# Normalization factors by way of DRAM, and channel-major groups kept in place, in the projection stage of a compacted pair-mixing layer

## The chip, the core and the metric

One core of a Trainium2 chip runs the whole program. Its engines work side by side, each through its own list of instructions in order: PE (matmuls and transposes, into PSUM), DVE and ACT (elementwise work and reductions), POOL (elementwise work, and DMAs that it issues in software), SP (here only a DMA queue). They wait for each other by semaphores. The metric is the time of one execution on the device in microseconds, as the median of the runs shown.

## What is computed

The reference has two layers on an image x of 512 x 512 places with 64 channels. The change lies in the first:

```python
xn = _ln(gn(x), norm_w, norm_b)          # over the 64 channels of each place
left  = (xn @ left_w  + left_b)  * mask
right = (xn @ right_w + right_b) * mask
left  = left  * sigmoid(xn @ lgate_w + lgate_b)
right = right * sigmoid(xn @ rgate_w + rgate_b)
out_gate = sigmoid(xn @ ogate_w + ogate_b)
out = einsum('bkjd,bkid->bijd', left, right)
x = x + (_ln(out, onorm_w, onorm_b) @ out_w + out_b) * out_gate
```

`gn` is a group norm over the whole image, in effect one scale and one shift per channel. `mask[i, j]` is `m[i] * m[j]`, with m a vector of zeros and ones, so left and right are nonzero only where both row and column are kept. The second layer adds a filter in a few Fourier modes of the result.

## The kernel before

When at most K = 256 of the 512 indices are kept, the kernel works on a compacted image. **Stage one** reads all of x, gathers statistics for the group norm, and keeps only the wanted columns in slots of one tile `xc`, of 128 partitions x 257 slots x 2 x 64: partition p and half r are row r * 128 + p of the compacted image, a slot is a column, and 64 channels lie beside each other.

**Stage two**, the slot projections, is where the change is (lines 694 to 786). It forms left and right for the 256 kept columns and writes them to `left_d` and `right_d` in DRAM, channel by channel. The work is in `groups = 64` groups q of four slots (`QB = 4` groups are one batch k). For each group:

- `channels`: four transposes of `xc` into PSUM (`xc_ps`), so that the two halves' channels lie on 128 partitions and the 128 rows of each slot beside each other (channel-major); ACT applies the group norm's scale and shift and writes the result to `gc_t`, one of `QB + 8 = 12` buffers.
- `centered`: four matmuls with a centering matrix turn the group back to rows on partitions, with the channel mean taken off (`cc_ps`, one buffer); ACT squares it (`sqc`), and DVE sums over channels (`total`). So there is one number per row, slot and half.
- `factors`: once per batch, nine short DVE steps on 128 x 32 numbers make the reciprocal root (`rq_out`); three steps are taken per iteration.
- `spread`: POOL copies each of a group's eight columns of factors 64 times (`rbc`, 128 x 512).
- `normed`: four transposes of `rbc` on PE give the factors channel-major in PSUM (`rc_ps`), and DVE multiplies `gc_t` by them (`xnc`).
- `project`: two matmuls of 64 channels each for the gates (`gates_c`), ACT's sigmoid (`sigc`, one buffer), two matmuls for the sides (`sides_c`), two DVE instructions that add the bias and multiply by the sigmoid (`o_c`, two buffers), and two DMAs on SP's queue that store 64 partitions each (256 KB) to `left_d` and `right_d`.

The order is written by hand (`manual_schedule`): a loop with a software pipeline, in which iteration q takes gates of group q, `normed` of q + 1, three root steps, `spread` of q + 2, `channels` of q + 10, `centered` of q + 9, sides and `o_c` of q, the sum over q + 9 and the stores of q. The loop runs from q = -10, so the first ten iterations only fill the pipeline, and in the last ones there is no channel work left. `xc_ps` has two PSUM buffers, `cc_ps`, `rc_ps`, `gates_c` and `sides_c` one each.

**After it** come the product over kept columns, which loads `left_d` and `right_d` (lines 829 to 856), a long stage that goes over the whole image again, and an end that is bound by DMA. None of them is touched, save that two small DVE products (`center_x`, `gate_x`, lines 803 and 804, in both kernels placed ahead of stage two's first sum by the planner) move to lines 818 and 819.

Of the kernel before, what the change touches and what calls it, by code (L numbers as in the profile page):

```python
# [9 lines left out]
F32 = mybir.dt.float32  # L10
I32 = mybir.dt.int32
AF = mybir.ActivationFunctionType
# [5 lines left out]
P = 128  # L18
N = 512
C = 64  # L20
# [11 lines left out]
K = 2 * P  # L32
AHEAD = 15
SHARE = 22
QB = 4
# [11 lines left out]
def conv_preact_kernel(ctx: ExitStack, tc: tile.TileContext, t: dict):  # L47
    nc = tc.nc
# [3 lines left out]
    dram = ctx.enter_context(tc.tile_pool(name="dram", bufs=1, space=DRAM))  # L52
# [14 lines left out]
    ident = load_const("c_ident", [P, P])  # L67
    center = load_const("c_center", [P, P])
# [13 lines left out]
    with tc.tile_pool(name="ix", bufs=1) as xp, tc.tile_pool(  # L82
        name="ixp", bufs=1, space=PSUM
# [529 lines left out]
    def compact(fc):  # L613
# [31 lines left out]
        with tc.tile_pool(name="xc", bufs=1) as cp:  # L645
            xc = cp.tile([P, K + 1, 2, C], F32, name="xc")
            with tc.tile_pool(name="f1", bufs=1) as sp, tc.tile_pool(name="f1x", bufs=2) as xp, tc.tile_pool(
                name="f1y", bufs=4
# [19 lines left out]
                for jc in range(NJ):  # L668
                    if jc % quarter == 0:
                        stats = sp.tile([P, 1, 16 * quarter, 6], F32, name="stats1c")  # L670
                    for r in range(4):
                        flat = xgs[jc][1][r].rearrange("p j c -> p (j c)")
                        for c in range(4):

                            ps = pt.tile([P, 4, P], F32, name="x_ps")
# [15 lines left out]
                ab1 = group_norm_affine(fc, sets, 2 * stats.shape[2], "xc")  # L691


            with tc.tile_pool(name="fb", bufs=QB + 8) as gp, tc.tile_pool(name="fw", bufs=2) as wk, tc.tile_pool(
                name="fr", bufs=3
            ) as rp, tc.tile_pool(name="fg", bufs=1) as sp, tc.tile_pool(name="fo", bufs=2) as op, tc.tile_pool(
                name="fpt", bufs=2, space=PSUM
            ) as pt, tc.tile_pool(name="fpc", bufs=1, space=PSUM) as pc, tc.tile_pool(
                name="fpp", bufs=1, space=PSUM
            ) as pp, tc.manual_schedule():  # L700
                groups = K // 4
                gts, totals, rss, rbs, xns, todo = {}, {}, {}, {}, {}, []

                def channels(q):
                    tps = pt.tile([P, 4, P], F32, name="xc_ps")
                    for i in range(4):
                        nc.tensor.transpose(tps[:, i, :], xc[:, 4 * q + i].rearrange("p r c -> p (r c)"), ident)
                    gts[q] = gp.tile([P, N], F32, name="gc_t")
                    nc.scalar.activation(
                        gts[q], tps.rearrange("p i k -> p (i k)"), AF.Identity, bias=ab1[:, 1:2], scale=ab1[:, 0:1]  # L710
                    )

                def centered(q):
                    cps = pc.tile([P, 8, C], F32, name="cc_ps")
                    for i in range(4):
                        nc.tensor.matmul(
                            cps[:, 2 * i : 2 * i + 2, :], gts[q][:, i * P : (i + 1) * P], center, start=True, stop=True
                        )
                    sq = wk.tile([P, 8, C], F32, name="sqc")
                    nc.scalar.activation(sq, cps, AF.Square)  # L720
                    k, n = divmod(q, QB)
                    if n == 0:
                        totals[k] = rp.tile([P, QB * 8], F32, name="total")
                    return sq, totals[k][:, 8 * n : 8 * n + 8]

                def factors(k):
                    rss[k], steps = rsqrt_steps(rp, totals.pop(k), 1.0 / C, EPS, [P, QB * 8])
                    todo.extend(steps)

                def spread(q):  # L730
                    k, n = divmod(q, QB)
                    rbs[q] = rp.tile([P, 8, C], F32, name="rbc")
                    nc.gpsimd.tensor_copy(rbs[q], rss[k][:, 8 * n : 8 * n + 8].unsqueeze(2).to_broadcast([P, 8, C]))  # L733

                def normed(q):
                    rps = pc.tile([P, N], F32, name="rc_ps")
                    flat = rbs.pop(q).rearrange("p (i r) c -> p i (r c)", r=2)
                    for i in range(4):
                        nc.tensor.transpose(rps[:, i * P : (i + 1) * P], flat[:, i, :], ident)
                    xns[q] = wk.tile([P, N], F32, name="xnc")  # L740
                    nc.vector.tensor_mul(xns[q], gts.pop(q), rps)

                def project(q, k):
                    ps = pp.tile([P, 2, N], F32, name=k + "_c")
                    for r in range(2):
                        h = slice(r * C, (r + 1) * C)
                        nc.tensor.matmul(ps[:, r, :], weights[k][h], xns[q][h], start=True, stop=True)
                    return ps


                for q in range(-QB - 6, groups):
                    live = lambda i: 0 <= q + i < groups
                    if live(0):
                        gates = project(q, "gates")
                        sig = sp.tile([P, 2, N], F32, name="sigc")
                        nc.scalar.activation(sig, gates, AF.Sigmoid, bias=biases["gates"])
                    if live(1):
                        normed(q + 1)
                    for step in todo[:3]:
                        step()  # L760
                    del todo[:3]
                    if live(2):
                        spread(q + 2)
                    if live(QB + 6):
                        channels(q + QB + 6)
                    if live(QB + 5):
                        sq, total = centered(q + QB + 5)
                    if live(0):
                        sides = project(q, "sides")
                        xns.pop(q)  # L770
                        res = op.tile([P, 4, 2, P], F32, name="o_c")
                        for r in range(2):
                            nc.vector.scalar_tensor_tensor(
                                res[:, :, r, :], sides[:, r].rearrange("p (i k) -> p i k", i=4), biases["sides"],
                                sig[:, r].rearrange("p (i k) -> p i k", i=4), ALU.add, ALU.mult,
                            )
                    if live(QB + 5):
                        nc.vector.tensor_reduce(total, sq, AX.X, ALU.add)
                        if (q + QB + 5) % QB == QB - 1:
                            factors((q + QB + 5) // QB)  # L780
                    if live(0):
                        for side, dst in enumerate((left_d, right_d)):
                            nc.sync.dma_start(
                                dst[:, 4 * q : 4 * q + 4, :].rearrange("c j k -> c (j k)"),
                                res[side * C : (side + 1) * C].rearrange("c j r k -> c (j r k)"),
                            )
# [20 lines left out]
        with tc.tile_pool(name="tri", bufs=1) as trp:  # L807
# [17 lines left out]
            with tc.tile_pool(name="ti", bufs=4) as ip, tc.tile_pool(name="tt", bufs=3) as tp, tc.tile_pool(  # L825
                name="tpt", bufs=4, space=PSUM
# [615 lines left out]
```

## Time and profile before

| what | us |
|---|---|
| median of 3 runs | 1835.98 (1834.19 to 1836.71) |
| profiled execution, device time | 1839.54 |
| its span, first to last instruction | 1837.7 |
| stage two: first channel transposes | 206.5 |
| first gates matmul | 227.62 |
| last o_c starts | 464.29 |
| last stores issued | 466.22 |
| next stage's first loads issued | 469.01 |

The granted clock of PE was 0.894 of full speed in the mean. In stage two it was 0.50 from 206 to 214 us, 0.85 from 214 to 218 and 1.00 from then on.

A line of the order of time is: start in us, duration in us, engine, line, instruction, the tile written and the tiles read, shape, how many instructions were merged, and in brackets idle time before and what ended it. Two instructions of one engine may overlap a little, so pace is read from start to start. A matmul in 32-bit floats shows as several records. The page's groups give busy time and mean duration by line; stretches give each engine's busy time between two moments, with the granted clock and the mean busy share of the 16 DMA engines.

### The profile page before, as it was taken

To read this page: it belongs to the slowest core of one execution; us is meant where nothing else is said; L and a number is where in the kernel's file an instruction comes from. 1 tells how busy PE (TensorE), PEld (TensorE's weight loads), DVE (VectorE), ACT (ScalarE), POOL (GpSimd) and SP (SyncE) were. 2 spreads that over 40 slices of the span, in tenths; PEclk is the share of its full clock that TensorE was granted. 3 is DMA by queue.
4 is the path that set the end of the run, shared out by engine and by line. 5 is a ranking of instruction groups with operands and counts; after the bars stand their busy time and mean duration, and the time that the engine had idled before them with its cause. 6 is when DMAs were issued, how large, how long until landed. Compare 5 with 4: busy or idle time off the path is not lost.

```text
span 1837.7 us, 33577 instructions
## 1 busy us (share of the span) xinstructions
PE 1637.7 (89%) x11414; PEld 1287.7 (70%) x11414; DVE 1423.6 (77%) x2973; ACT 961.9 (52%) x1708; POOL 945.3 (51%) x711
## 2 busy tenths in 40 slices
PE   6779799999799999999999999999999866998772
PEld 5667666665678878897788888888888744665441
DVE  5989777777455547788999999999999975675552
ACT  3555555555222259976777777777777631111000
POOL 3666211111000006788999999999999862211110
PEclk9989899999899999999999999999999966555555
DMA  6999255556656513667777876776777698999999
GB/s 255 381 375 371 106 127 138 138 138 154 208 174 182 177 41 141 224 234 257 254 244 249 279 269 233 241 274 234 253 258 258 210 273 338 411 426 426 427 427 379
DMA packets 188453, 467.94 MB, mean 255 GB/s; under 512 B 34672, under 2 KB 134000, under 8 KB 147184
## 3 DMA queue, kind: packets, MB, share of 16 engines
q1 hardware_dynamic: 157376, 262.21, 42.5%
q0 software_dynamic: 27712, 201.40, 29.1%
q10 hardware_dynamic: 3184, 2.08, 0.4%
q8 instruction: 93, 1.52, 0.3%
q14 instruction: 88, 0.72, 0.1%
HBM read 278.05 MB, written 187.56 MB: 253 GB/s over the span
## 4 chain that ended last, share of the span: by engine, by line
PE 29%; DVE 16%; DMA 9%; POOL 4%; issue 3%; ACT 1%; DVEq 0%; POOLq 0%; ACTq 0%
PE c_ps L979 6%; PE w_ps L979 6%; PE t_ps L969 5%; PE l_ps L1348 4%; DVE stats2c L1097 4%; DMA places<-x_h,dst_i 4%; PE y_ps L990 4%; DVE z_t L1195 3%; DVE scratch L1012 3%; DVE z_t L1201 3%; PE f_ps L1069 2%; POOL z_t L1038 2%; DMA out_x<-places 2%; POOL places L1042 2%; DMA lx_t<-x_h,dst_i 2%
## 5 line engine op out<-in xcount | busy, mean ns | idle before, releaser
L979 PE MATMUL w_ps<-gate_x,xt_c 128*128 128x128 f32 x2048 | 280.1, 280 | 32.1 <-DVE z_t L1195 26.7
L1042 POOL TENSOR_TENSOR places<-places,z_t 128x1024 f32<-128x1024 f32 x127 | 301.2, 2371 | 8.0
L979 PEld LDWEIGHTS w_ps<-gate_x,xt_c 128*128 128x128 f32 x2048 | 251.5, 194 | 47.8 <-DVE z_t L1195 43.4
L979 PE MATMUL c_ps<-center_x,xt_c 128*128 128x128 f32 x2048 | 276.2, 278 | 1.2 <-ACT xt_c L1008 0.6
L979 PEld LDWEIGHTS c_ps<-center_x,xt_c 128*128 128x128 f32 x2048 | 252.1, 194 | 3.9 <-ACT xt_c L974 2.3
L1348 PE MATMUL l_ps<-places,rinv 24*128 24x512 f32 x512 | 207.8, 1124 | 29.3 <-DVE places L1355 18.6
L1097 DVE BATCH_NORM_STATS2 stats2c<-places 128x6 f32<-128x128 f32 x1024 | 220.5, 278 | 12.5 <-POOL places L1042 12.5
L1012 DVE TENSOR_REDUCE scratch<-sq_c 128x16 f32<-128x1024 f32 x160 | 194.6, 1216 | 27.9 <-ACT sq_c L1007 18.7
L1146 ACT ACTIVATE z_t<-z_t 128x1024 f32<-128x1024 f32 x128 | 135.5, 1059 | 133.7 <-DVE z_t L1201 116.0
L1199 POOL TENSOR_TENSOR z_t<-z_t,bias_row_out 128x1024 f32<-128x1024 f32 x32 | 75.7, 2365 | 246.6 <-DVE z_t L1195 242.5
L969 PE MATMUL t_ps<-c_ident,places 128*128 128x128 f32 x1280 | 199.0, 278 | 1.3 <-DVE places L854 1.3
L1348 PEld LDWEIGHTS l_ps<-places,rinv 24*128 24x128 f32 x512 | 120.3, 303 | 111.9 <-DVE places L1355 59.6
L969 PEld LDWEIGHTS t_ps<-c_ident,places 128*128 128x128 f32 x1280 | 144.5, 142 | 60.6 <-issue 50.3
L974 ACT ACTIVATE xt_c<-t_ps,ab_xc 128x512 f32<-128x512 f32 x256 | 176.0, 687 | 10.7 <-PE t_ps L969 9.8
L1195 DVE TENSOR_TENSOR z_t<-w_ps,rs_n 128x512 f32<-128x512 f32 x256 | 171.9, 672 | 3.7 <-PE w_ps L979 3.5
L1004 ACT ACTIVATE sq_c<-c_ps 128x512 f32<-128x512 f32 x256 | 150.5, 588 | 30.9 <-PE c_ps L979 29.4
L679 DVE BATCH_NORM_STATS2 stats1c<-x_ps 128x6 f32<-128x512 f32 x256 | 155.6, 681 | 12.5 <-PE x_ps L678 12.2
L1201 DVE TENSOR_TENSOR z_t<-z_t,scratch 128x1024 f32<-128x1024 f32 x128 | 156.3, 1221 | 10.0 <-ACT rs_n L1018 3.8
L1038 POOL TENSOR_TENSOR z_t<-z_t,places 128x1024 f32<-128x1024 f32 x64 | 151.6, 2369 | 16.2 <-ACT z_t L1146 13.3
L1355 DVE TENSOR_TENSOR places<-places,l_ps 128x512 f32<-128x512 f32 x176 | 110.2, 683 | 56.1 <-DMA places<-x_h,dst_i 45.5
L1038 POOL TENSOR_TENSOR z_t<-z_t,bias_row_out 128x1024 f32<-128x1024 f32 x63 | 149.4, 2371 | 4.6 <-ACT z_t L1146 4.0
L733 POOL COPY rbc<-rq_out 128x512 f32<-128x512 f32 x64 | 38.3, 613 | 210.0 <-DVE rq_out L209 132.0
(212 smaller groups left out, 2748.8 us busy)
## 6 DMA issues: line engine op xcount, KB each, us to landing
x_h<-places SPq DMA_DIRECT2D x64, 1024.0 KB
out_x<-places SPq DMA_DIRECT2D x44, 1024.0 KB
places<-u_d SPq DMA_DIRECT2D x512, 64.0 KB
out_x<-lx_t SPq DMA_DIRECT2D x20, 1024.0 KB
left_d<-o_c SPq DMA_DIRECT2D x64, 256.0 KB
right_d<-o_c SPq DMA_DIRECT2D x64, 256.0 KB
left_raw<-left_d SPq DMA_DIRECT2D x64, 256.0 KB
right_raw<-right_d SPq DMA_DIRECT2D x64, 256.0 KB
```

The costliest lines, as they stand in the source:

```text
L679: nc.vector.bn_stats(stats[:, 0, 16 * (jc % quarter) + 4 * r + c, :], ps.rearrange("p i k -> p (i k)"))
L969: nc.tensor.transpose(tps[:, i, :], flat[:, o : o + P], ident)
L974: nc.scalar.activation(xts[s], tps, AF.Identity, bias=ab1[:, 2:3])
L979: nc.tensor.matmul(ps[:, 2 * i : 2 * i + 2, :], xts[s][:, i, :], w, start=True, stop=True)
L1004: nc.scalar.activation(sq, cps, AF.Square)
L1012: nc.vector.tensor_reduce(totals[k % 2][:, 8 * (n - 1) : 8 * (n + 1)], sqs.pop(s // 2), AX.X, ALU.add)
L1038: nc.gpsimd.tensor_mul(zs[k, c], zs[k, c], u)
L1042: nc.gpsimd.tensor_add(xr, xr, zs.pop((k, c)))
L1097: nc.vector.bn_stats(st[k // 4][:, g, k % 4, :], x_of(k)[:, :, 2 * g : 2 * g + 2])
L1195: nc.vector.tensor_mul(z[:, 8 * odd : 8 * odd + 8, :], wps, rs)
L1201: nc.vector.tensor_add(z, z, bias_ps["ogate"].unsqueeze(1).to_broadcast([P, 16, C]))
L1348: nc.tensor.matmul(ps.rearrange("p j o -> p (j o)"), rinv[h, b, :], it[h], start=True, stop=True, tile_position=(32 * g, 0),)
```

## The change

Three things change in stage two.

1. The channel-major group is written by ACT over the four slots of `xc` it came from, and no longer to a buffer of its own: `gts(q)` is a view of `xc`. The pool of twelve buffers goes.
2. The factors take another way. `spread` is now done once per batch. PE transposes the 128 x 32 factors (one transpose, `rc_ps`, 32 x 128), ACT copies them to SBUF (`turned_c`) and issues four DMAs, one per group, that write them to a DRAM tensor `rs_d`, so that for each group and each half r the 512 factors lie in one row. Then POOL issues two DMAs, one per half, each of which reads the four rows of that half and writes them to 64 partitions (`rbc`, 128 x 4 x 512, two buffers). `normed` multiplies by that tile; POOL's copies and PE's four transposes per group are gone.
3. The pipeline is longer: `lead = QB + 8 = 12`. Iteration q takes `channels` of q + 13 and `centered` of q + 12, and the loop starts at q = -13. `spread` of batch k stands in iteration 4k - 5, after `channels` and before `centered`; the batch's first `normed` stands in iteration 4k - 1. On ACT the order in such an iteration is sigmoid, channel activation, copy, four DMA issues, square.

The diff, cut to what matters:

```diff
+            rs_d = dram.tile([K // 4, 2, 4 * P], F32, name="rs_d")
-            with tc.tile_pool(name="fb", bufs=QB + 8) as gp, tc.tile_pool(name="fw", bufs=2) as wk, tc.tile_pool(
+            with tc.tile_pool(name="fn", bufs=2) as np_, tc.tile_pool(name="fw", bufs=2) as wk, tc.tile_pool(
+                def gts(q):
+                    return xc[:, 4 * q : 4 * q + 4].rearrange("p i r c -> p (i r c)")
...
-                    gts[q] = gp.tile([P, N], F32, name="gc_t")
                     nc.scalar.activation(
-                        gts[q], tps.rearrange("p i k -> p (i k)"), AF.Identity, bias=ab1[:, 1:2], scale=ab1[:, 0:1]
+                        gts(q), tps.rearrange("p i k -> p (i k)"), AF.Identity, bias=ab1[:, 1:2], scale=ab1[:, 0:1]
                     )
...
-                def spread(q):
+                def spread(k):
+                    ps = pc.tile([QB * 8, P], F32, name="rc_ps")
+                    nc.tensor.transpose(ps, rss.pop(k), ident)
+                    turned = np_.tile([QB * 8, P], F32, name="turned_c")
+                    nc.scalar.copy(turned, ps)
+                    groups_d = rs_d[k * QB : (k + 1) * QB]
+                    for n in range(QB):
+                        nc.scalar.dma_start(
+                            groups_d[n].rearrange("r (i p) -> i r p", p=P), turned[8 * n : 8 * n + 8]
+                        )
+                    rbs[k] = np_.tile([P, QB, N], F32, name="rbc")
+                    for r in range(2):
+                        h = slice(r * C, (r + 1) * C)
+                        nc.gpsimd.dma_start(
+                            rbs[k][h], groups_d[:, r].unsqueeze(0).to_broadcast([C, QB, N])
+                        )
+
+                def normed(q):
                     k, n = divmod(q, QB)
-                    rbs[q] = rp.tile([P, 8, C], F32, name="rbc")
-                    nc.gpsimd.tensor_copy(rbs[q], rss[k][:, 8 * n : 8 * n + 8].unsqueeze(2).to_broadcast([P, 8, C]))
-
-                def normed(q):
-                    rps = pc.tile([P, N], F32, name="rc_ps")
-                    flat = rbs.pop(q).rearrange("p (i r) c -> p i (r c)", r=2)
-                    for i in range(4):
-                        nc.tensor.transpose(rps[:, i * P : (i + 1) * P], flat[:, i, :], ident)
                     xns[q] = wk.tile([P, N], F32, name="xnc")
-                    nc.vector.tensor_mul(xns[q], gts.pop(q), rps)
+                    nc.vector.tensor_mul(xns[q], gts(q), rbs[k][:, n])
...
-                for q in range(-QB - 6, groups):
+                lead = QB + 8
+                for q in range(-lead - 1, groups):
...
-                    if live(2):
-                        spread(q + 2)
-                    if live(QB + 6):
-                        channels(q + QB + 6)
-                    if live(QB + 5):
-                        sq, total = centered(q + QB + 5)
+                    if live(lead + 1):
+                        channels(q + lead + 1)
+                    if live(lead - QB) and (q + lead - QB) % QB == QB - 1:
+                        spread((q + lead - QB) // QB)
+                    if live(lead):
+                        sq, total = centered(q + lead)
...
-                    if live(QB + 5):
+                    if live(lead):
                         nc.vector.tensor_reduce(total, sq, AX.X, ALU.add)
-                        if (q + QB + 5) % QB == QB - 1:
-                            factors((q + QB + 5) // QB)
+                        if (q + lead) % QB == QB - 1:
+                            factors((q + lead) // QB)
```

More of the change, by code (lines that the diff above doesn't have):

```diff
@@ L701, in compact @@
                 groups = K // 4
-                gts, totals, rss, rbs, xns, todo = {}, {}, {}, {}, {}, []
+                totals, rss, rbs, xns, todo = {}, {}, {}, {}, []
+                def gts(q):
+                    return xc[:, 4 * q : 4 * q + 4].rearrange("p i r c -> p (i r c)")
                 def channels(q):
@@ L716, in centered @@
                         nc.tensor.matmul(
-                            cps[:, 2 * i : 2 * i + 2, :], gts[q][:, i * P : (i + 1) * P], center, start=True, stop=True
+                            cps[:, 2 * i : 2 * i + 2, :], gts(q)[:, i * P : (i + 1) * P], center, start=True, stop=True
                         )
```

## The prediction

> **What bounds the kernel now.** I read the slices and the chain of waits first. The chain is spread thinly over the whole kernel, and no line of the stage that the change touches is among those it names. So I went to that stage. The projection loop starts with the first channel transposes at 206.3 us, its first gates matmul runs at 227.62, and its last o_c starts at 464.29. The stretches view (busy us and count of each engine, granted clock, DMA share) shows three parts: a fill, 54 full iterations, and a tail without channel work.
>
> ```profile
> core 0: us, PE busy (x) PEld busy (x) DVE busy (x) ACT busy (x) POOL busy (x), PEclk, DMA share, GB/s
> ...
> 206.00:229.00 23.00, 20.27 (x125) 17.22 (x126) 10.93 (x37) 13.38 (x20) 2.34 (x4) 0.80 0.00 1
> ...
> 250.00:400.00 150.00, 150.00 (x940) 97.12 (x940) 115.43 (x245) 88.97 (x119) 23.96 (x40) 1.00 0.55 138
> ...
> 432.00:467.00 35.00, 31.48 (x149) 13.66 (x148) 27.27 (x54) 13.89 (x14) 4.79 (x8) 1.00 0.68 167
> ```
>
> In the middle PE is busy in all of 150 us at the full clock. As a matmul's end is modelled, I checked it with starts, in the order of time of one iteration (start, duration, engine, line):
>
> ```profile
> 303.37 0.77 ACT L709 ACTIVATE gc_t<-xc_ps,ab_xc 128x512 f32<-128x512 f32 x1
> ...
> 303.43 1.13 PE L747 MATMUL sides_c<-xnc,w_sides 64*128 64x512 f32 x4
> ...
> 304.03 0.59 ACT L720 ACTIVATE sqc<-cc_ps 128x512 f32<-128x512 f32 x1
> 304.39 1.02 PE L747 MATMUL gates_c<-xnc,w_gates 64*128 64x512 f32 x4
> ...
> 304.66 1.41 DVE L773 SCALAR_TENSOR_TENSOR o_c<-sides_c,b_sides,sigc 128x512 f32<-128x512 f32 x2 [0.70 <-ACT sqc L720]
> ...
> 305.35 0.66 PE L739 MATMUL rc_ps<-c_ident,rbc 128*128 128x128 f32 x4
> ...
> 305.84 0.60 PE L707 MATMUL xc_ps<-c_ident,xc 128*128 128x128 f32 x4
> ...
> 306.19 1.11 ACT L756 ACTIVATE sigc<-gates_c,b_gates 128x1024 f32<-128x1024 f32 x1 [1.56 <-DVE o_c L773]
> ...
> 306.28 1.06 PE L716 MATMUL cc_ps<-c_center,gc_t 128*128 128x128 f32 x8
> ...
> 307.26 1.13 PE L747 MATMUL sides_c<-xnc,w_sides 64*128 64x512 f32 x4
> ...
> 308.23 1.02 PE L747 MATMUL gates_c<-xnc,w_gates 64*128 64x512 f32 x4
> ```
>
> From start to start: gates 0.96, rc_ps 0.49, xc_ps 0.44, cc_ps 0.98, sides 0.97, together 3.84 us without a hole (3.83 over many iterations). **PE sets the pace.** Behind it, DVE needs 1.33 (two o_c) + 0.59 (total) + 0.59 (xnc) + up to 0.61 (three root steps) = 3.12, ACT 1.01 + 0.66 + 0.49 = 2.16. In the tail the loop is o_c to sides to o_c: 1.41 + 0.15 + 1.24 = 2.80 (455.94, 458.74, 461.51 are o_c starts).
>
> **The change part by part.**
>
> *Leaving PE:* the four rc_ps transposes of each group, 0.49 us. What is next? DVE at 3.12 and the tail's 2.80 are both under 3.34, so the full iteration falls to 3.84 - 0.49 = 3.34 by my rounding. POOL's copies (613 ns each) go too; PE's matmuls never waited for one in the iterations above, so they are worth nothing. The product xnc reads its factor from SBUF instead of PSUM: I keep 0.59, since DVE has 0.2 to spare.
>
> *Coming to PE:* one transpose of 32 columns per four groups, 0.11 (a quarter of 0.44).
>
> *Coming to ACT:* in one iteration of four, between the channel activation and sqc, a copy of 32x128 out of PSUM, and four DMA issues that wait for it. The copy: rows of 64 columns take 0.31 and of 256 take 0.47, so about 0.35. Hand-over 0.1. The nearest row for the issues is ACT's own four stores of few partitions, and it is back to back:
>
> ```profile
> 1468.40 1.80 ACTq L1091 DMA_DIRECT2D modes_d<-places  x4
> ```
>
> So 0.45 each, 1.80. Other issues of the trace bound it: 0.33 (small constants on ACT) to 0.60 (right_d on SP). Sum 0.35 + 0.1 + 1.8 = 2.25 us in which ACT does nothing else. Queued behind is sqc, and cc_ps has one buffer, so the next group's centering waits for sqc. With the gates' start at 0: o_c of the group before starts at 0.28 and frees ACT for sigc at 1.81; channel activation 2.82; copy 3.48; sqc 3.48 + 2.25 = 5.73, done 6.37 with its hand-over. PE would be there at 3.34 + 0.11 + 0.96 + 0.44 = 4.85. **PE stands for 1.5 us** in every such iteration; it is the bound, so that is never made up. With issues of 0.33 it is 1.0, with 0.60 it is 2.1. Lane waits of these issues lie on stores of three to four iterations earlier, long landed.
>
> *The factor's new road:* copy, four writes to DRAM, two loads on POOL's queue. The writes: the last stores are issued until 466.82 and the next stage's loads stop waiting for them at 469.01, so 2.2 us. POOL has no other work here. Its issue is 0.59 by this row, and a 1 MB gather on its queue lands in 5.8 us at the median, beside other traffic:
>
> ```profile
> 467.17 0.59 POOL L798 DMA_DIRECT2D u_d<-bias_row_out  x1 [14.72 <-DVE bias_row_out L797]
> ...
> places<-in_x,src_i POOLq DMA_INDIRECT x64, 5.8
> ...
> q1 hardware_dynamic: 7652, 25.10, 55.0%
> ```
>
> Here is a rule against the change. The Trainium skill, SBUF — State Buffer, section "Door 1: The DMA port swizzle", says that 64 partitions reach only 8 of 16 ports (196 GB/s measured there), and its section "Can I just issue two DMAs to hit both halves?" that two transfers to the two halves do not add up. By the row, the pair of loads (1 MB) lands 5.8 us after its issue; by the rule, an estimate of 2 x 0.52 MB / 196 GB/s = 5.3 us of pure movement plus about 2 of fixed cost, 7.3, before anything shares the engines. The trace sides with the rule: the last row above (queue, packets, MB, share, over 250 to 432 us) is the half-partition stores, 55% of 16 engines for 25.1 MB, 15.8 GB/s per busy engine, against 427 GB/s at a full share (27 each) for whole-height transfers near the end. The loads add 1 MB per four groups: share 1.05 MB / (16 x 15.8 GB/s) = 4.2 us of some 14.9, 28% on top of the stores' 8.4 (56%). It fits, but not loosely; I take 8 us for the pair. From the copy: 2.25 + 2.2 + 8 = 12.5 us. The first xnc that needs it stands four iterations on: 4 x 3.34 plus the 1.6 that PE loses, less 1.3, since in its iteration the copy stands at 3.48 and xnc at 2.2: 13.7. In time by 1 us. The ends are 5.8 and 12 (twice half the bytes, each at half the rate of the row); each us beyond 9 costs one us per load.
>
> *The longer lead:* the fill grows from 10 to 13 iterations, and the tail without channel work from 10 to 13. Total PE work is the same. But the first factor now takes the long road with little beside it. Before, centerings come every 1.84 us and gates start at 227.62. Spread 0 stands in the iteration of the eighth centering (its channel activation is at 224.31), so copy 225.0, issued 227.2, written 229.4, loads with no stores beside them 6.5, 235.9, xnc 0.68: **gates start at about 236.6, 9.0 us later.** PE fills four more groups in that time and then rests some 2 us. Would that halve the clock? Before this stage PE was nearly idle from 202 to 206 and ran at 0.50 until about 215. TensorE: Matmul & The Clock Gate, Part 1, puts the limit at an idle window of about 3.4 us; by it the rest is free, by the trace's case it could cost up to 4 us. I take 0.
>
> *In place of gc_t:* ACT writes over slots whose transposes it has waited for anyway. 0.
>
> **The sum,** from first gates to last o_c. Before: 236.7 (54 x 3.83 + 10 x 2.87 + 1.2). After: 51 x 3.34 = 170.3; 12 spreads x (0.11 + 1.5) = 19.3; tail 13 x 2.80 = 36.4; its two loads have only 4 x 2.8 us of lead and come about 2 us late each, 4; rest 1.2. That is 231.2, 5.5 better. The start is 9.0 worse: **3.5 us slower**, and half a us for stores that share the engines with loads: 4. Later stages do not change. The profiled execution took 1839.54 us (span 1837.7), 3.6 over the median of 1835.98; I add 4 to both: 1843.5, and 1840 at the median.
>
> **The rivals.**
>
> *ACT pays less than its rows say (0.27).* If four tiny issues take 0.2 to 0.33 each, PE stands 0.5 to 1.0 and not 1.5; 12 x 0.5 to 1.0 plus a us at either end: 8 to 14 better than the forecast, 1826 to 1832. For it: each writes only 4 KB. Against: no ACT issue in the trace is under 0.33.
>
> *The load becomes the bound (0.27, the slower side).* Place: the first xnc of each four groups, DVE waiting for the pair, o_c behind it, PE for xnc. Point: pair later than 9 us. At 11 us it is 2 us x 14 loads = 28 more, 1868; at 10, 1854. For it: half ports, 84% of the engines' time wanted, 64 reads of the same rows, which no row here shows. Against: 1 us of slack, and waiting stretches its own lead.
>
> *It does nothing that counts:* not possible for PE's part, since the transposes are gone.
>
> **How the numbers follow.** Forecast case 0.46: 1832 to 1848 alone, 1840 at its centre. A measurement here can tell about 0.2%, 3.7 us, from no change, so this case is split between same (0.22) and slower (0.21), with 0.03 faster. Rivals: 0.25 faster and 0.02 same; 0.27 slower. Together faster 0.28, same 0.24, slower 0.48. The range 1826 to 1862 takes in the cheap issues and half of the late loads.
>
> **What would show it.** Right: gates of full iterations 3.34 apart, one in four about 1.5 longer with PE waiting for sqc; turned_c and four ACT issues of 0.45 before it; first gates near 236; DVE not waiting for rbc except at the first load and in the tail. Wrong: iterations evenly 3.3 apart (cheap issues), or DVE waiting at every fourth xnc for DMA (late load), or a clock below 1.0 after the first wait.

## The result, and the profile after

| | before | after |
|---|---|---|
| median of 4 runs, us | 1835.09 (1833.35 to 1836.71) | 1891.99 (1890.45 to 1892.96) |
| ratio | 1 | 1.0308 [1.0294, 1.0321] |
| span of the profiled execution | 1837.7 | 1890.5 |
| first gates matmul | 227.62 | 237.26 |
| last o_c starts | 464.29 | 521.35 |
| granted clock, mean | 0.894 | 0.885 |

The changed kernel is 3.1% slower, outside the predicted range. The last o_c comes 57 us later, as much as the medians lost (56.9; the spans of the two profiled executions differ by 52.8): all of the loss lies in stage two. From its first transposes to its last o_c the stage takes 315.3 us for 257.8. The stretches view of the changed kernel, with the same columns as before (fill, full iterations, end of the stage):

```profile
206.00:237.00 31.00, 22.48 (x151) 19.14 (x151) 13.25 (x44) 15.87 (x27) 1.34 (x2) 0.89 0.16 35
250.00:400.00 150.00, 124.84 (x675) 73.36 (x673) 98.52 (x207) 76.99 (x110) 9.83 (x16) 0.94 0.67 174
467.00:525.00 58.00, 40.13 (x133) 14.06 (x132) 32.43 (x63) 17.52 (x19) 3.01 (x5) 0.84 0.70 186
```

PE had no hole in 150 us before; now it is busy in 125 of them, and the granted clock, 1.00 before, is 0.94. So two things are new: PE stands, and when it runs it is partly at half speed. The order of time around one spread (L739 is the copy, L742 the four issues on ACT, L798 the stores):

```profile
343.60 1.06 PE L720 MATMUL cc_ps<-c_center,xc 128*128 128x128 f32 x8
...
345.57 0.24 ACT L739 COPY turned_c<-rc_ps 32x128 f32<-32x128 f32 x1
...
345.84 2.80 ACTq L742 DMA_DIRECT2D rs_d<-turned_c  x4
346.50 0.66 PE L712 MATMUL xc_ps<-c_ident,xc 128*128 128x128 f32 x4
...
348.68 0.60 ACT L724 ACTIVATE sqc<-cc_ps 128x512 f32<-128x512 f32 x1 [2.87 <-DMA rs_d<-turned_c]
...
349.33 2.07 PE L720 MATMUL cc_ps<-c_center,xc 128*128 128x128 f32 x8 [2.18 <-ACT sqc L724]
...
351.34 1.75 PE L761 MATMUL sides_c<-xnc,w_sides 64*128 64x512 f32 x4
...
351.94 1.23 POOL L748 DMA_DIRECT2D rbc<-rs_d  x2 [17.00 <-DMA rs_d<-turned_c]
352.93 1.02 PE L761 MATMUL gates_c<-xnc,w_gates 64*128 64x512 f32 x4
```

The four issues hold ACT for 2.80 us, sqc comes behind them, and the next cc_ps waits 2.18 us for it. The same matmuls that took 1.06 at 343.60 then take 2.07, and the sides 1.75 instead of 1.13. That is the half clock, in plain durations: from 349.20 to 352.64 the granted clock is 0.50. From the start of that cc_ps to the start of gates it is 3.60 us; without a pause it is 0.98 + 0.97 = 1.95.

The waits of 237 to 525 us (engine, line, what it waited for; us in total, times, longest); then the page's row of the loads (count, size, median us to landing); then, from the view of the tile rs_d, ACT's issues (count, min/median/max ns of one, first and last start):

```profile
ACT sqc L724 <- DMA rs_d<-turned_c: 36.3, 12, 3.6
...
PE cc_ps L720 <- ACT sqc L724: 29.7, 12, 3.3
...
DVE o_c L788 <- DMA right_d<-o_c: 16.2, 7, 3.9
...
DVE xnc L755 <- DMA rbc<-rs_d: 3.5, 2, 2.3
```

```profile
rbc<-rs_d POOLq DMA_DIRECT2D x32, 512.0 KB, 6.9
```

```profile
L742 ACTq DMA_DIRECT2D rs_d<-turned_c x64: 589/598/1221, 224.1 to 494.6; - x64
```

The loads land 6.9 us after their issue and DVE waited for one only twice, so the new road itself is in time. What is late is ACT (12 times, as often as there are spreads among full iterations) and, in the third row, stores: o_c has two buffers, and a store that lands late keeps both engaged. Between 250 and 470 us the queue of the loads takes 24.7% of the DMA engines' time beside 41.7% for that of the stores; before, the stores had the engines to themselves.

Single iterations that are free of both take 3.4 us (o_c to o_c 3.41, 3.39, 3.47 at the start of the stage), but the one in four with the spread takes 5.5 to 8.8.

### The profile page after: what moved, and what is told of

Read it like the earlier page. It is cut to its first block, busy times and chain, and to the rows that moved or that the text cites. A ratio compares the mean times of both kernels' runs of the same rounds, so it can differ in the third digit from the quotient of the medians.

```text
span 1890.5 us, 33128 instructions
## 1 busy us (share of the span) xinstructions
PE 1639.7 (87%) x11174; PEld 1272.9 (67%) x11174; DVE 1425.5 (75%) x2973; ACT 965.2 (51%) x1724; POOL 927.8 (49%) x679
## 4 chain that ended last, share of the span: by engine, by line
PE 43%; DVE 22%; DMA 15%; issue 5%; POOL 4%; ACT 4%; ACTq 2%; SPq 1%; POOLq 0%; DVEq 0%
PE tri_c_ps L865 7%; PE w_ps L994 5%; PE c_ps L994 5%; DMA places<-x_h,dst_i 4%; PE t_ps L984 4%; DMA out_x<-places 4%; DVE stats2c L1112 4%; DVE stats1c L679 4%; PE y_ps L1005 4%; DVE scratch L1027 4%; DVE z_t L1210 4%; DVE z_t L1216 3%; PE l_ps L1363 3%; PE sides_c L761 3%; PE cc_ps L720 3%
## 5 line engine op out<-in xcount | busy, mean ns | idle before, releaser
L1019 ACT ACTIVATE sq_c<-c_ps 128x512 f32<-128x512 f32 x256 | 150.6, 589 | 31.3 <-PE c_ps L994 29.7
L748 POOL DMA_DIRECT2D rbc<-rs_d x32 | 19.8, 623 | 277.9 <-DVE rq_w L202 139.7
```

## The experiments

Two theories at first. **A:** the issues on ACT hold back sqc, PE stands, and the pause costs the clock. **B:** the loads to 64 partitions delay the stores, and o_c waits for buffers. All diffs are against the changed kernel unless another is named; the times of the kernel before beside these runs were 1833.5 to 1836.2.

### The four issues on SP instead of ACT

```diff
-                        nc.scalar.dma_start(
+                        nc.sync.dma_start(
```

> The changed kernel takes 1892 us. Theory A: the four issues on ACT (0.6 us and more each, not 0.45) hold back sqc, PE stands at cc_ps for about 2.4 us per batch, and then runs part of the next iterations at half clock. Theory B: the loads of rbc share the DMA engines with the stores, and o_c waits for right_d. Here the four issues go to SP's queue. A: no pause at cc_ps, clock 1.00, ordinary and spread iterations alike at 3.4 us, about 1840 us. B: the waits of o_c for right_d stay or grow (16 us in the changed kernel), 1870 us or more.

Measured: 1875.02 us, ratio 1.0219 [1.0191, 1.0248]. The waits of its stage two (237 to 500 us):

```profile
DVE o_c L788 <- DMA right_d<-o_c: 52.9, 21, 5.0
```

The wait of sqc for the issues is gone, and the wait for stores has grown from 16 to 53 us. The issues cost the same on SP (median 582 ns), where the stores are queued behind them. The wait only moved. That stores are late is B's sign, but not all of the growth need be B's: in the spread around 338 us the four issues hold SP's queue until 340.73, and the store of an o_c that ended at 339.80 is issued only at 340.83. This run does not part the two.

### One issue for a batch

The sums are laid out with the half r outermost, so that all 32 partitions go to DRAM as one piece of 16 KB; the loads then read one row of 8 KB per partition instead of four of 2 KB.

```diff
-            rs_d = dram.tile([K // 4, 2, 4 * P], F32, name="rs_d")
+            rs_d = dram.tile([K // 4 // QB, 2, QB * 4 * P], F32, name="rs_d")
...
-                    return sq, totals[k][:, 8 * n : 8 * n + 8]
+                    return sq, totals[k].rearrange("p (r n i) -> p n i r", r=2, n=QB)[:, n]
...
-                    for n in range(QB):
-                        nc.scalar.dma_start(
-                            groups_d[n].rearrange("r (i p) -> i r p", p=P), turned[8 * n : 8 * n + 8]
-                        )
+                    nc.scalar.dma_start(rs_d[k].rearrange("r (j p) -> (r j) p", p=P), turned)
...
-                            rbs[k][h], groups_d[:, r].unsqueeze(0).to_broadcast([C, QB, N])
+                            rbs[k][h].rearrange("p n k -> p (n k)"), rs_d[k, r : r + 1].to_broadcast([C, QB * N])
```

> One DMA of 32 partitions (16 KB) on ACT in place of four of 8 (4 KB each), columns of the sums ordered so that it is contiguous; loads read one row of 8 KB per partition instead of four of 2 KB. If the price is per issue (theory A): one issue of 0.6 us, PE's pause at cc_ps shrinks to 0.2 us, clock 1.00, about 1840 us. If it goes by bytes or rows: 2.5 us for the one, and 1890 us. Theory B: as in the run with SP, 1870 us or more.

Measured: 1846.12 us, ratio 1.0059 [1.0042, 1.0076]. From the view of rs_d and from the waits:

```profile
L740 ACTq DMA_DIRECT2D rs_d<-turned_c x16: 308/308/357, 222.0 to 449.7; - x16
```

```profile
DVE o_c L784 <- DMA right_d<-o_c: 27.5, 12, 4.4
```

A quarter as many issues, each half as long: 0.31 us per batch instead of 2.4 to 3.6. With the loads' longer rows, which come with it, that brings 46 us. What is left above the kernel before is B's: the waits for stores have grown from 16 to 27.5 us.

### Loads of a quarter of the bytes

Only the first group's factors of each batch are loaded and used for all four; the output changes.

```diff
-                    rbs[k] = np_.tile([P, QB, N], F32, name="rbc")
+                    rbs[k] = np_.tile([P, 1, N], F32, name="rbc")
...
-                            rbs[k][h], groups_d[:, r].unsqueeze(0).to_broadcast([C, QB, N])
+                            rbs[k][h], groups_d[:1, r].unsqueeze(0).to_broadcast([C, 1, N])
...
-                    nc.vector.tensor_mul(xns[q], gts(q), rbs[k][:, n])
+                    nc.vector.tensor_mul(xns[q], gts(q), rbs[k][:, 0])
```

> Each load brings only the first group's factors of a batch (a quarter of the bytes), and all four groups use them, so the output differs; the issues on ACT stay. Theory A: only the waits of o_c for right_d go (16 us at most), pauses at cc_ps and the half clock stay: 1876 to 1888. Theory B: 40 us or more go, 1850 or less.

Measured: 1866.84 us, ratio 1.0177 [1.0155, 1.0198]. The waits of its stage two:

```profile
ACT sqc L724 <- DMA rs_d<-turned_c: 34.3, 13, 2.9
...
PE cc_ps L720 <- ACT sqc L724: 24.0, 13, 2.5
```

There is no row of o_c waiting for right_d any more, and ACT's is as it was. So the loads are what delays the stores, and ACT's wait does not come from them. The loads land after 3.7 us, and 25 us are gained (23 in the traces, from the stage's first transposes to the last o_c).

### Four buffers for o_c

```diff
-            ) as rp, tc.tile_pool(name="fg", bufs=1) as sp, tc.tile_pool(name="fo", bufs=2) as op, tc.tile_pool(
+            ) as rp, tc.tile_pool(name="fg", bufs=1) as sp, tc.tile_pool(name="fo", bufs=4) as op, tc.tile_pool(
```

> One number is changed against the changed kernel: o_c has four buffers instead of two, so that a store may land 6 us later before anyone waits for it. The four issues on ACT stay. Theory A (ACT's four issues of 0.6 hold back sqc, PE stands and then runs at half clock; the waits for stores come only from what this shifts): the waits of o_c for right_d (16 us in all) go, but the next wait in line, ACT's sqc, takes most of it: 1880 to 1890, clock stays under 0.93. Theory B (loads to 64 partitions slow the stores, o_c waits for them, and this is what makes the spread iterations long): spread iterations fall under 5.5 and the time to 1855 to 1870.

Measured: 1873.97 us, ratio 1.0218 [1.0196, 1.0239]; the waits for right_d are gone here too, sqc still waits 34.4 us for its issues, and the clock from 250 to 450 is 0.86 to 0.93. Eighteen us of the loss are bought back with two more buffers. The time lies between the two expectations, 4 us above B's; what is left is A's, since the iterations with a spread still take 5.5 to 8.1 us.

### One issue and four buffers

Both edits together.

> One issue per batch (contiguous rows, 32 partitions, 0.31 us) and four o_c buffers together. If ACT's issues and late stores are all there is to the loss, both with the half clock as their consequence: no wait of o_c for right_d, clock near 1.0 from 218 on, iterations 3.4 throughout with one in four at 3.6, and the end of the stage at 471 to 474 minus the fill: 51 x 3.4 + 13 x 2.8 + 12 x 0.2 after gates at 237.3 = 449 to 455, so 1815 to 1826, faster than the kernel before. If the loads take something else (DVE waits for rbc, or the stores' queue is full and even four buffers run out), it stays at 1838 to 1846.

Measured: 1823.65 us (1818.37 to 1828.55), ratio 0.9938 [0.9918, 0.9959]: 0.6% under the kernel before. A stretch of full iterations, and the spread in it:

```profile
300.00:350.00 50.00, 50.00 (x300) 30.97 (x300) 43.20 (x91) 33.84 (x48) 4.09 (x8) 1.00 0.83 227
```

```profile
343.72 0.24 ACT L739 COPY turned_c<-rc_ps 32x128 f32<-32x128 f32 x1
...
343.99 0.31 ACTq L740 DMA_DIRECT2D rs_d<-turned_c  x1
...
344.34 0.60 ACT L724 ACTIVATE sqc<-cc_ps 128x512 f32<-128x512 f32 x1 [0.39 <-ACT turned_c L739]
344.68 0.66 PE L712 MATMUL xc_ps<-c_ident,xc 128*128 128x128 f32 x4
345.17 1.06 PE L720 MATMUL cc_ps<-c_center,xc 128*128 128x128 f32 x8
```

PE is busy in 50 of 50 us at the full clock, and sqc is ready before PE comes to cc_ps. All full iterations take 3.37 to 3.53 us, the spread's too, with the DMA share at 0.83. The two causes together are the whole loss, and 11 us of gain that they had hidden.

### What makes an issue cost 0.6

In place of the one issue: four issues of 8 partitions, each to consecutive rows of DRAM (against the kernel with one issue and four buffers).

```diff
-                    nc.scalar.dma_start(rs_d[k].rearrange("r (j p) -> (r j) p", p=P), turned)
+                    flat_d = rs_d[k].rearrange("r (j p) -> (r j) p", p=P)
+                    for n in range(QB):
+                        nc.scalar.dma_start(flat_d[8 * n : 8 * n + 8], turned[8 * n : 8 * n + 8])
```

> As the kernel with one issue and four o_c buffers, but the 16 KB are written by four issues of 8 partitions each, every one to consecutive rows of DRAM (4 KB in one piece). The loads stay as there (one row of 8 KB per partition). If the price lies in the number of issues and their 8 partitions, four take 2.4 us or more, PE stands 1.5 to 3 us per batch and the time goes back to about 1870, where the four strided issues with four buffers were (1874). If it lies in the scattered form of the writes, or if the gain came from the loads' longer rows, four take 1.2 us at most and the time stays within 10 of 1824.

Measured: 1834.59 us, ratio 1.0003 [0.9993, 1.0013]. The view of rs_d and the order of time:

```profile
L742 ACTq DMA_DIRECT2D rs_d<-turned_c x64: 267/315/923, 223.5 to 442.2; - x64
```

```profile
338.30 1.51 ACTq L742 DMA_DIRECT2D rs_d<-turned_c  x4
...
340.50 1.16 PE L720 MATMUL cc_ps<-c_center,xc 128*128 128x128 f32 x8 [0.83 <-ACT sqc L724]
```

Same bytes, same number of issues and of partitions: 315 ns instead of 598, PE waits 0.83 us instead of 2.2, and cc_ps behind it stays at 1.16. This kernel still differs from the one with the old issues and four buffers (1873.97) in the form of the loads (and in the order of the sums, which the consecutive form needs). So, against that one, the same two-dimensional stores with the loads' long rows:

```diff
-                            groups_d[n].rearrange("r (i p) -> i r p", p=P), turned[8 * n : 8 * n + 8]
+                            rs_d[k][:, n * N : (n + 1) * N].rearrange("r (i p) -> i r p", p=P), turned[8 * n : 8 * n + 8]
...
-                            rbs[k][h], groups_d[:, r].unsqueeze(0).to_broadcast([C, QB, N])
+                            rbs[k][h].rearrange("p n k -> p (n k)"), rs_d[k, r : r + 1].to_broadcast([C, QB * N])
```

> The four scattered issues of the changed kernel (each writes eight pieces of 512 bytes, those of one half 512 bytes apart, the two halves in different rows), four o_c buffers, and the loads of the cheap kernels (one row of 8 KB per partition instead of four of 2 KB). It parts the two things in which the kernel with four consecutive issues (1834.6) differs from the one with four scattered issues and four buffers (1874). If the form of the writes is the price: issues of 0.6 again, four take 2.5 to 3.5 us, clock under 0.95, and 1860 to 1875. If the loads' form was: issues below 0.4 or the pause hidden, and 1835 to 1845.

Measured: 1870.55 us, ratio 1.0202 [1.0183, 1.0221], issues of 597 ns at the median. The price is that of the form of the writes. In the changed kernel the half r is innermost on the partitions and outermost in DRAM, so the eight pieces of 512 bytes of a group go out in two dimensions; where partitions and addresses run in the same order, they are one piece of 4 KB. That is worth 36 us. Why this form holds the queue longer stays open; a permuted order alone does not fix the price, since ACT's stores to modes_d, which the prediction read at 0.45, are permuted too. The loads' form makes them land sooner, 5.3 us after issue for 7.0, but of its worth in time nothing can be told (3.4 us against 1873.97, with the intervals of the ratios overlapping).

### The half clock by itself

When does it come? Read in short stretches, the granted clock of the changed kernel changes only at moments that lie multiples of 3.41 us apart: down at 315.08, 332.16, 349.20 and 386.74, and up 3.4 us after each. Cut at such moments, with the columns as before (the second number of a row is PE's busy time):

```profile
362.86:366.27 3.41, 1.99 (x12) 0.75 (x8) 1.54 (x3) 0.97 (x3) 0.00 (x0) 1.00 0.70 174
366.27:369.68 3.41, 2.24 (x14) 1.65 (x16) 1.75 (x5) 2.76 (x4) 0.24 (x1) 1.00 0.55 138
...
400.40:403.82 3.42, 1.57 (x12) 0.89 (x9) 1.65 (x3) 1.12 (x2) 0.00 (x0) 1.00 0.64 135
403.82:407.23 3.41, 3.41 (x13) 2.08 (x13) 1.34 (x6) 1.75 (x3) 1.23 (x2) 0.50 0.41 123
```

PE's pause of 2.59 us before 367.44 is shared by two windows, which lack 1.42 and 1.17 us of PE work, and costs nothing. Its pause of 1.85 us before 403.35 lies in one window, and the next window runs at half clock. Counted so, from 216 to 522 us in all fourteen traces of this case, none of 980 full-speed windows that lacked less than 1.68 us was followed by one at half clock, all 54 that lacked more than 1.88 us were, and between these 40 of 54. So where a pause falls decides as well as its length. What this costs was tried with filler.

The pause is filled with transposes of a constant, in the iteration in which PE waits for sqc. A first version put twenty of them into the spread's own iteration, and the pause is in the next.

```diff
-                    ps = pc.tile([QB * 8, P], F32, name="rc_ps")
+                    bank = pc.tile([P, N], F32, name="rc_ps")
+                    ps = bank[: QB * 8, :P]
                     nc.tensor.transpose(ps, rss.pop(k), ident)
+                    for _ in range(20):
+                        nc.tensor.transpose(bank[:, P : 2 * P], ident, ident)
```

> The changed kernel with 20 transposes of a constant (about 2.2 us of PE work that nothing uses) put into each pause, between the factors' transpose and the next centering. If the half clock after a pause is a cost of its own: clock 1.00 in the stage, and 20 to 28 us less, 1865 to 1872, although PE has 35 us more work. If the clock does not matter: 1892, or up to 10 more where the work outlasts the pause.

It took 1889.59 us, ratio 1.0303, with the clock at 0.98. As the filler did not stand in the pause, it added PE work as well, and settles nothing. In its right place:

```diff
                     if live(lead):
+                        if q > -QB and q % QB == 0:
+                            bank = pc.tile([P, N], F32, name="rc_ps")
+                            for _ in range(20):
+                                nc.tensor.transpose(bank[:, P : 2 * P], ident, ident)
                         sq, total = centered(q + lead)
```

> Twenty transposes of a constant (2.35 us at full clock) ahead of the centering of the iteration after each spread, where PE stands 2.2 to 3.3 us for sqc. They take PE time that is idle anyway. If the half clock after these pauses costs what the rows show (cc_ps 2.07 for 1.06, sides 1.77 for 1.13, some 1.5 to 2 us per spread), the mean clock of the stage rises to 0.97 or more and the time falls by 12 to 25: 1867 to 1880. If the clock matters little because ACT's issues and the stores set the pace of these iterations, the clock rises and the time stays within 5 of 1892.

Measured: 1893.58 us, ratio 1.0315 [1.0293, 1.0336]: the clock was 1.00 from 250 to 400 us and nothing was gained. By itself that would say that the clock is free. But here o_c waits for stores as well, 22.4 us in its stage two against 16.2 before the filler, so what PE gains is waited for again; and at the start the filler had no pause to fill and set the first o_c back by 2.3 us (counted from the stage's first transposes, which come anywhere from 201.8 to 208.1 us in the traces). So it was tried once more where stores hold nothing up: on the kernel with two-dimensional issues, long rows and four buffers (1870.55), with 18 transposes and not before the fifth full iteration.

```diff
+                        if q > 0 and q % QB == 0:
+                            bank = pc.tile([P, N], F32, name="rc_ps")
+                            for _ in range(18):
+                                nc.tensor.transpose(bank[:, P : 2 * P], ident, ident)
                         sq, total = centered(q + lead)
```

> As the kernel with four scattered issues, four o_c buffers and the loads' long rows (1870.6), in which no o_c waits for a store any more; only PE's pause of 1.8 to 2.6 us for sqc in each batch is left. It is filled with 18 transposes of a constant (2.1 us at full clock), from the fifth full iteration on. What this brings is the price of the half clock by itself. Where the pause was 2.1 us, centering and sides took 3.6 us from start to gates' start instead of 2.06, so 1.5 us for each of some 10 to 12 batches: 1850 to 1858 with the clock at 0.98 or more and the pauses of sqc unchanged. If the half clock costs nothing because ACT or DVE sets the pace of these iterations anyway, 1868 to 1873.

Measured: 1860.31 us (1856.06 to 1865.08), ratio 1.0128 [1.0098, 1.0157]. A spread in it:

```profile
348.97 2.50 ACTq L742 DMA_DIRECT2D rs_d<-turned_c  x4
...
350.16 2.13 PE L785 MATMUL rc_ps<-c_ident 128*128 128x128 f32 x18
351.52 0.60 ACT L724 ACTIVATE sqc<-cc_ps 128x512 f32<-128x512 f32 x1 [2.58 <-PE rc_ps L785]
352.18 1.16 PE L720 MATMUL cc_ps<-c_center,xc 128*128 128x128 f32 x8
353.26 1.13 PE L761 MATMUL sides_c<-xnc,w_sides 64*128 64x512 f32 x4
```

ACT is as late as without the filler (sqc waits 2.58 us; the row names PE's filler as the releaser, but sqc starts as the four issues end, 348.97 + 2.50). Work behind the pause now runs at full speed: iterations with a spread take 5.5 us, nearly all of them, instead of 5.5 to 8.1. The time falls by 10 us (by the ratios 0.0074, 14 us), a little less than expected; from first to last o_c it is 244.2 instead of 258.6, 14 less, while the first o_c came 3.8 later, since the whole stage began that much later (207.03 for 203.24). Ten windows at half clock lay between the first o_c and 450 us without the filler, none with it until 448 us; at 1.7 us of PE's time each, 17 us is an estimate of the most that they could cost. So the half clock costs 10 to 14 us where PE sets the pace, and next to nothing where stores do.

### A shorter start and end

On the kernel with one issue and four buffers, the first batch's first group is loaded ahead of the other three.

```diff
+                    cuts = (0, 1, QB) if k == 0 else (0, QB)
+                    for a, b in zip(cuts, cuts[1:]):
+                        for r in range(2):
...
+                                rbs[k][h, a:b].rearrange("p n k -> p (n k)"),
+                                rs_d[k, r : r + 1, a * N : b * N].to_broadcast([C, (b - a) * N]),
```

> As the kernel with one issue and four o_c buffers, but the first batch's factors are loaded in two steps, the first group alone ahead (2 x 128 KB), then the other three. The start is bound by this road: the first gates matmul at 234.0 waited 2.3 us for the load. A quarter load landed 3 us sooner than a whole one, less one more pair of issues ahead of the other three groups: gates at 231.5 to 232.5, and the time 1 to 2.5 us shorter than the kernel without it, 1821 to 1823, too little to tell apart in time alone. If the other three groups then come late (their loads are issued 1 us later, their first reader stands 3.4 us later than the first group's), DVE waits at the second xnc instead and nothing is gained.

Measured: 1814.73 us (1812.81 to 1820.12), ratio 0.9892 [0.9876, 0.9909]. The first gates start at 231.00 instead of 234.01; the second xnc then waits 1.30 us for the rest, and the last o_c comes at 446.04 instead of 449.35. But in this trace the whole stage began 1.7 us sooner (first transposes at 204.35 for 206.03), ahead of anything that the edit touches: counted from there, the gates come 1.3 us sooner and the last o_c 1.6. The medians differ by 8.9, so 1.6 is shown and the rest is not explained. The same split for the last two batches:

```diff
-                    cuts = (0, 1, QB) if k == 0 else (0, QB)
+                    cuts = (0, 1, QB) if k in (0, 14, 15) else (0, QB)
```

> As the kernel that loads the first batch's first group ahead, with the same split for the last two batches, whose loads came 0.9 to 1.6 us late in the tail, where an iteration takes 2.8 us. A quarter load lands 3 us sooner, so these three waits (3.7 us in all) should go, unless the other three groups, issued 1 us later, are late in their place. 1811 to 1815 if they go; within 1 us of the kernel without it if they only move.

Measured: 1815.83 us (1811.41 to 1817.12), ratio 0.9897 [0.9882, 0.9913]. The wait of batch 14 went (2.77 for 3.59 us between o_c); that of batch 15 moved (4.35, 3.33 and 3.30 after 4.37, 3.72 and 2.78). No gain that can be told. These two are the fastest versions found, about 1% under the kernel before.

## Why the prediction was wrong

"Slower" was forecast for the start alone: from first gates to last o_c the stage was to gain 5.5 us, and it lost 47 (284.1 for 236.7). The path there was right, from ACT's issues over sqc to a standing PE. Three terms on it were too small: the price of an issue, the clock (put at nothing) and the stores (put at half a us).

**Where the 57 us come from.** Each row has one edit more than the row above it; the last column is one execution, from the stage's first transposes to its last o_c:

| kernel | us | step | stage in the trace |
|---|---|---|---|
| changed kernel | 1891.99 | | 315.3 |
| four o_c buffers | 1873.97 | -18.0 | 296.6 |
| and long rows for the loads | 1870.55 | -3.4 | 294.3 |
| and consecutive instead of two-dimensional writes | 1834.59 | -36.0 | 259.3 |
| and one issue instead of four | 1823.65 | -10.9 | 243.3 |

The steps add up to 68, the loss and the 11 us by which the last kernel is under the one before. The last two, 47 us, are what ACT's issues cost with pauses and clock, where the prediction had 18 (12 x 1.5).

**PE's part: right.** Full iterations were to be 3.34 and are 3.4 wherever nothing is late; the kernel with both causes removed runs at that pace in all its full iterations.

**The start: right.** Gates at 237.26 for 236.6; counted from the first transposes they come 10.1 us later than before, for the 9.0 forecast.

**The road: right, with the margin larger than thought.** The loads land after 6.9 us for the 8 taken; DVE waited for them 3.5 us in all. (The 15.8 GB/s per busy engine come out as 15.7 from the row they were read from, which changes no sum.) The rival "the load becomes the bound" named the right resource and the wrong victim: the loads did not come late, they made the stores late.

**"So 0.45 each, 1.80": too little.** The row it was read from, ACT's own stores of few partitions, has another form of destination. The issues cost 0.598, which is the dear end of the bounds given, and with it the prediction's own working gave PE 2.1 us of standing; the iteration shown above has 2.18, the mean of twelve is 29.7 / 12 = 2.5. For this term alone that is 12 x (2.5 - 1.5) = 12 us. The cheap issues of the first rival do exist, at 0.315, with consecutive writes; with four o_c buffers as well, that kernel ran even with the one before, at 1834.6.

**"I take 0" for the clock: a failed step.** The question was put for the rest at the start, and never for the twelve pauses that the same text priced at 1.5 us. Nine of the twelve were followed by the half clock, worth 10 to 14 us in a kernel where no o_c waits for a store. The prediction cited the Trainium skill, TensorE: Matmul & The Clock Gate, Part 1, for an idle window of about 3.4 us. The traces agree with the 3.41 us, and not with a window that is idle throughout: here one that lacked 1.83 us of PE work could bring the half clock. At the start, too, the rest was not free: it left the window before 236.58 with 2.02 us of standing, and the first iteration ran at half clock. The measurement decides: a pause of 1.8 us can cost the clock, and one of 3.03 in the changed kernel's fill, which two windows shared, did not.

**"Half a us for stores that share the engines": the other failed step.** The share of the engines was added up (84%) and called enough, and it was: the kernel at 1823.65 moves the same bytes at 0.83 of the engines' time. But the sum says nothing of when a single store lands. With two buffers, o_c must have the store of two iterations ago landed, and in every fourth iteration two loads of 512 KB come in between; the 18 us are that wait. The prediction named what is queued behind each new instruction on ACT, and not what is queued behind each new transfer.

Beyond the 231.2 us that the prediction gave the stage from first gates to last o_c, 284.1 were measured: 53 more. The issues' size (12), the half clock (14 at most) and the stores (18) make 44; 3 more are the first iteration, at half clock after the wait for the first load (6.7 us from gates to o_c for 3.8 in the kernel at 1823.65). About 6 stay unassigned, and since each wait hides part of another, the terms are not strictly to be added.

## What to carry to other kernels

A DMA issue on a compute engine's queue is an instruction of that engine, and its price follows the form of its access pattern before its bytes: lay the data out so that one consecutive piece goes out, and check what is queued behind. When a new stream of transfers is added, look up the buffer depth of every other stream on the same engines, and not only the sum of their shares. And an edit that removes a cause and brings little (the issues on SP, the clock's filler) does not show that the cause is cheap while another wait stands ready in the same iteration: here the filler brought 10 us once the stores were out of the way. A pause of PE has two prices, its length and the clock after it; the second is read from the granted clock, window by window.

## What the runs showed of the hardware

- A 4 KB write from 8 partitions costs its queue 598 ns when its eight pieces of 512 bytes stand in DRAM in another order than on the partitions, 315 when in the same; 16 KB from 32 partitions in one consecutive piece cost 308. The first form cost nearly the same on SP (582).
- The granted clock changed only at multiples of 3.41 us. A window of that length at full speed that lacked less than 1.68 us of PE work was never followed by half clock (0 of 980), one that lacked more than 1.88 us always (54 of 54). At half clock the eight matmuls of cc_ps took 2.07 us for 1.06.
- Two loads of 512 KB to 64 partitions each, of factors that are read 64 times from the same rows, landed 6.9 us after issue at the median, beside stores; with a quarter of the bytes 3.7. Beside stores at full pace, in the kernel at 1823.65, it was 7.8.
